# Two Mamba stages and a ConvLSTM: the first direction's softplus summed on TensorE, B and C spread through DRAM, five pairs in two chunks with B on GpSimd

## The chip, the cores and the metric

The kernel runs on one core of a Trainium2 chip. The time is the device time of one execution in microseconds (us): 7586.24, the median of three runs (7583.68 to 7590.27). Engines are named as in the profile: PE (TensorE), DVE (VectorE), ACT (ScalarE), POOL (GpSimd), SP (SyncE, which here only issues transfers).

## The reference, cut to what matters

The input x is 1 x 64 x 256 x 128 in float32 (channels, time, frequency). Layer 0 runs two Mamba stages, one along time (L = 256) and one along frequency (L = 128), each with a forward and a backward direction. Layer 1, a convolutional LSTM, follows; the change doesn't touch it. For each sequence a direction computes, with d = 128 inner channels and 16 states s:

```python
xz = einsum(rmsnorm(u), in_proj);  x, z = split(xz)
x = silu(causal_conv4(x))
dt, B, C = split(einsum(x, x_proj), [4, 16, 16])
dt = softplus(einsum(dt, dt_proj) + dt_b)
for t:                                    # a scan along the sequence
    h = exp(dt[t] * A) * h + dt[t] * B[t] * x[t]      # h is d x s
    y[t] = sum_s(h * C[t])
out = einsum((y + x * Dp) * silu(z), out_proj) + u
```

## The kernel before

A stage works through 64 chunks of 512 tokens (2 sequences of 256, or 4 of 128). The 128 x 16 = 2048 rows of h of one direction are cut into 16 groups of 128 partitions (8 channels by 16 states). Two groups make a **pair**, a tile of 128 x 1024; a direction has 8 pairs, a chunk 16: pairs 0 to 7 of the first direction, 8 to 15 of the second. All engines run through one hand-written order (`run`, L561): a step S for every pair, and in it, in this order,

- `times_b(S + 1)` (L454): the PSUM tile `bx` times B, on DVE. For the pairs in `SWAPPED` (L61, numbers modulo 32, so over two chunks) ACT copies `bx` to the SBUF tile `dA` and writes the decays into `bx` instead, and POOL does the product[...]
- `recur(S)` (L464): the scan itself, one DVE instruction of 128 x 1024; after the last pair of a direction `gate` (L509), y times silu(z) on DVE
- `outputs(S - 1)` (L482): h times C on POOL
- `inputs(S + 2)` (L421): four pairs of matmuls that spread dt * x to the rows of the pair, into one of three `bx` tiles
- `decays(S + 2)` (L435): ACT's exp(A * rep), two instructions, into one of four `dA` tiles; in slot 5 of a chunk the decays of S + 2 and of S + 3 are done, in slot 6 none
- what `HEAD` (L68) has for this slot
- `add_up(S - 2)` (L487), every second step: PE sums h * C over the states.

`HEAD` is the list of what prepares a chunk: (slot, function, arguments). Slots count steps from the first pair of the chunk **before** the one prepared; slot 16 is the prepared chunk's first pair, and a slot of 18 or -4 falls together with slot 2 or 12 of the neighbouring chunk. The steps of one slot run in the list's order, an older chunk's ahead of a younger one's. Each engine takes its own instructions strictly in this order.

The way of one chunk through `HEAD`: `squares`, `means`, `rms`, `normalise` (L305: xn on POOL, then four transfers of 64 KB into `unp`, SBUF to SBUF); `project_x` and `project_z` on PE, ACT copies to `xs` and `zs`; `silus` (L340) in slot 5 with a change of ACT's table before and after; then for each direction d

- `softplus_a`, `softplus_b` (L349, L363): the matmul with Wdt, then six ACT passes. `softplus_c`, `softplus_d`: dt = relu + log w + (e + w), three adds on POOL
- `dt_away` (L380): dt to DRAM (`there`), four transfers of 64 KB
- `spread_dt` (L400): four times 1 MB from `there` to `rep`, where a partition holds the dt of its channels; three `rep` tiles, each used by two pairs
- `times_x` (L387): dtx = dt * xs on POOL
- `project_bc` (L392): B and C, already spread over 128 partitions, by matmuls with weights in which each of the 16 columns stands eight times, and ACT copies from PSUM.

All transfers are issued by SP, in this same order. Matmuls of the head share one PSUM tile (`mm`, L273), so each waits until ACT has read the one before.

Of the kernel before, what the change touches and what calls it, by code (L numbers as in the profile page):

```python
# [29 lines left out]
F32 = mybir.dt.float32  # L30
# [6 lines left out]
P = 128  # L37
# [3 lines left out]
NS = 16  # L41
NBC = 2 * NS
DL = P // NS
# [3 lines left out]
NTOK = 512  # L47
# [10 lines left out]
NRING = 4  # L58
NH = 5
LAG = 2  # L60
SWAPPED = (5, 21, 29)  # L61
EXP_AND_LN = "natural_log_exp_and_others"
SILU = "silu_and_others"
EDGES = (0, 1, LF - 2, LF - 1)
# [2 lines left out]

HEAD = (  # L68
    (-12, "load"),
    (-7, "squares"),  # L70
    (-6, "means"),
    (-6, "rms"),
    (-6, "normalise"),
    (0, "project_x", 0),
    (1, "project_z", 0),
    (4, "project_x", 1),
    (5, "project_z", 1),
    (5, "silus"),
    (7, "softplus_a", 0),
    (7, "softplus_b", 0),  # L80
    (9, "softplus_c", 0),
    (9, "project_bc", 0, 1),
    (10, "softplus_d", 0),
    (10, "dt_away", 0),
    (11, "softplus_a", 1),
    (11, "spread_dt", 0, 0),
    (12, "times_x", 0),
    (12, "project_bc", 1, 1),
    (12, "project_bc", 0, 0),
    (12, "spread_dt", 0, 1),  # L90
    (13, "softplus_b", 1),
    (13, "project_bc", 1, 0),
    (14, "spread_dt", 0, 2),
    (15, "softplus_c", 1),
    (16, "softplus_d", 1),
    (16, "spread_dt", 0, 3),
    (17, "dt_away", 1),
    (18, "spread_dt", 1, 0),
    (20, "times_x", 1),
    (20, "spread_dt", 1, 1),  # L100
    (22, "spread_dt", 1, 2),
# [4 lines left out]
class Mamba:  # L106


    def __init__(self, ctx, tc, d):
        nc = tc.nc  # L110
        self.nc, self.tc = nc, tc
        cp = ctx.enter_context(tc.tile_pool(name="m_const", bufs=1))
# [47 lines left out]
        nc.scalar.activation(self.A, self.A, AF.Exp)  # L160
        nc.vector.tensor_scalar(self.A, self.A, -1.0, None, ALU.mult)

        self.G1, self.G2, self.Wz, self.Wdt, self.Wb, self.Wc, self.Dd, self.W2 = ([] for _ in range(8))
        self.W3, self.lin_b = [], []
        with tc.tile_pool(name="m_prep", bufs=2) as pp, tc.tile_pool(
            name="m_prep_ps", bufs=2, space=PSUM
        ) as ps:
            lins = []
            for i, n in enumerate(("tlin", "flin")):
                lin = pp.tile([C, 2, C], F32, name=n, tag=n, bufs=1)  # L170
                nc.sync.dma_start(out=lin, in_=d[n + "_w"].rearrange("(h i) o -> i h o", h=2))
                lins.append(lin)
                b = cp.tile([C, 1], F32, name=n + "b", tag=n + "b")
                nc.sync.dma_start(out=b, in_=d[n + "_b"].rearrange("(c o) -> c o", o=1))
                self.lin_b.append(b)

                w3 = cp.tile([P, 2, C], F32, name=f"w3{i}", tag=f"w3{i}")
                nc.vector.memset(w3, 0.0)
                nc.vector.tensor_add(w3[0:C, 0], lin[:, 0], lin[:, 1])
                nc.vector.tensor_add(w3[0:C, 0], w3[0:C, 0], self.ident[0:C, 0:C])  # L180
                nc.vector.tensor_copy(w3[C:P, 1], w3[0:C, 0])
                self.W3.append(w3)

            for i in range(4):
                win = pp.tile([C, 2 * P], F32, name="win", tag="win")
                nc.sync.dma_start(out=win, in_=d["in_proj"][i])
                cw = pp.tile([C, 4, P], F32, name="cw", tag="cw")
                nc.sync.dma_start(out=cw, in_=d["conv_w"][i].partition_broadcast(C))
                xpd = pp.tile([RANK, P], F32, name="xpd", tag="xpd")
                nc.sync.dma_start(out=xpd, in_=d["x_proj_dt"][i])  # L190
                dtw = pp.tile([RANK, P], F32, name="dtw", tag="dtw")
                nc.sync.dma_start(out=dtw, in_=d["dt_proj"][i])
                xbc = pp.tile([P, NBC], F32, name="xbc", tag="xbc")
                nc.sync.dma_start(out=xbc, in_=d["x_proj_bc"][i])
                ow = pp.tile([C, P], F32, name="ow", tag="ow")
                nc.sync.dma_start(out=ow, in_=d["out_proj"][i])

                nc.vector.tensor_scalar(win, win, normw[:, i : i + 1], None, ALU.mult)
                wz = cp.tile([C, P], F32, name=f"wz{i}", tag=f"wz{i}")
                nc.vector.tensor_copy(wz, win[:, P : 2 * P])  # L200
                self.Wz.append(wz)

                taps = ((3, 2), (1, 0)) if i % 2 == 0 else ((2, 3), (0, 1))
                for j, keep in enumerate((self.G1, self.G2)):
                    g = cp.tile([P, P], F32, name=f"g{j}{i}", tag=f"g{j}{i}")
                    nc.vector.tensor_mul(g[0:C], win[:, 0:P], cw[:, taps[j][0]])
                    nc.vector.tensor_mul(g[C:P], win[:, 0:P], cw[:, taps[j][1]])
                    keep.append(g)

                pw = ps.tile([P, P], F32, name="pw", tag="pw")  # L210
                nc.tensor.matmul(pw, lhsT=xpd, rhs=dtw, start=True, stop=True)
                wdt = cp.tile([P, P], F32, name=f"wdt{i}", tag=f"wdt{i}")
                nc.vector.tensor_copy(wdt, pw)
                self.Wdt.append(wdt)

                for h, keep in ((0, self.Wb), (1, self.Wc)):
                    w = cp.tile([P, NS, DL], F32, name=f"wbc{h}{i}", tag=f"wbc{h}{i}")
                    nc.vector.tensor_copy(
                        w, xbc[:, h * NS : (h + 1) * NS].unsqueeze(2).to_broadcast([P, NS, DL])
                    )  # L220
                    keep.append(w.rearrange("p s d -> p (s d)"))

                dd = cp.tile([P, P], F32, name=f"dd{i}", tag=f"dd{i}")
                nc.vector.tensor_scalar(dd, self.ident, dp[:, i : i + 1], None, ALU.mult)
                self.Dd.append(dd)

                po = ps.tile([P, C], F32, name="po", tag="po")
                nc.tensor.matmul(po, lhsT=ow, rhs=lins[i // 2][:, i % 2], start=True, stop=True)
                w2 = cp.tile([P, C], F32, name=f"w2{i}", tag=f"w2{i}")
                nc.vector.tensor_copy(w2, po)  # L230
                self.W2.append(w2)


class Stage:
# [142 lines left out]
    def softplus_d(self, ch, d):  # L377
        self.nc.gpsimd.tensor_add(self.at["dt", d], self.at["lw", d], self.at["dt", d])  # L378

    def dt_away(self, ch, d):  # L380

        there = self.dram.tile([32, 4, NTOK], F32, name="there", tag="there")
        for r in range(4):
            self.nc.sync.dma_start(out=there[:, r], in_=self.at["dt", d][32 * r : 32 * r + 32])
        self.at["there", ch, d] = there
# [3 lines left out]
        self.nc.gpsimd.tensor_mul(dtx, self.at["dt", d], self.at["xs", ch, d])  # L389
        self.at["dtx", ch, d] = dtx  # L390

    def project_bc(self, ch, d, h):  # L392
        wt = (self.m.Wb, self.m.Wc)[h][2 * self.stage + d]
        pb = self.mm("pb")
        self.nc.tensor.matmul(pb, lhsT=wt, rhs=self.at["xs", ch, d], start=True, stop=True)  # L395
        t = self.wk.tile([P, NTOK], F32, name="bc", tag=f"bc{h}", bufs=3)
        self.nc.scalar.copy(t, pb)  # L397
        self.at["BC"[h], ch, d] = t

    def spread_dt(self, ch, d, k):  # L400
# [28 lines left out]
        self.at["bx", S] = bx  # L429

    def swapped(self, S):

        return S % 32 in SWAPPED

# [711 lines left out]
```

## Time and profile before

| engine | busy us | share | what most of it is |
|---|---|---|---|
| DVE | 7263.6 | 96% | scans (L472) and products with B (L462) |
| POOL | 6916.1 | 91% | h times C (L485) 4806.7, B of swapped pairs (L459) 453.5, four softplus and dtx passes of about 327 each |
| PE | 6523.0 | 86% | bx (L428), sums over states (L500), B and C (L395) 655.8 |
| ACT | 5568.8 | 73% | decays (L450), copies of B and C (L397) 294.4 |
| transfers | - | 68.9% of 16 engines | rep (L403), 1024 of 1 MB |

The two Mamba stages fill the span up to about 6900 us, the ConvLSTM the rest. A line of a group reads: line, engine, operation, output<-input, shapes, count; busy us and mean ns of one; idle time ahead of it, and what ended it. In a timeline a line reads: start in us from the span's start, duration (of a merged row: from its first start to its last end), engine, line, operation, count, and in brackets how long the engine was idle and for what. SPq is SP's queue of transfers; its rows show the issue, not the landing.

### The profile page before, as it was taken

Reading aid. Unit: us, or ns where it says so; the run is one execution under the profiler, and the core shown is the slowest. Engines: PE = TensorE matmul, PEld = TensorE weight load, DVE = VectorE, ACT = ScalarE, POOL = GpSimd, SP = SyncE. Lnnn points to the kernel's source line nnn. Section 1 sums busy time; section 2 is a strip of 40 time slices with the busy share of each in tenths; the row PEclk is TensorE's granted clock in tenths of the full one; section 3 lists DMA queues with packets and bytes.
Section 4 is the critical chain, followed back from the end, with each engine's and each line's share of the span. In section 5 each row is a group of like instructions: output and inputs, shape, how many; then the busy total and the mean of one; then the engine's idle time right before and its main releaser. Section 6 shows DMA issues by size and latency. Waiting matters only on the chain.

```text
span 7581.6 us, 83087 instructions
## 1 busy us (share of the span) xinstructions
PE 6523.0 (86%) x24588; PEld 2179.7 (29%) x24588; DVE 7263.6 (96%) x5008; ACT 5568.8 (73%) x10188; POOL 6916.1 (91%) x3860
## 2 busy tenths in 40 slices
PE   6888888888888888887988888888888888888999
PEld 2222222222222222221222222222222222225887
DVE  6999999999999999997999999999999999996887
ACT  5778777777777877775787877878778787774333
POOL 6999999999999999996999999999999999995554
PEclk9999999999999999998999999999999999999999
DMA  5777877777777777775778777777777777772000
GB/s 131 175 178 175 183 174 177 174 174 182 176 181 174 174 182 177 180 173 124 184 182 186 171 176 172 171 181 172 178 173 171 179 171 179 172 172 77 15 15 17
DMA packets 276049, 1208.67 MB, mean 159 GB/s; under 512 B 46704, under 2 KB 104720, under 8 KB 144528
## 3 DMA queue, kind: packets, MB, share of 16 engines
q1 hardware_dynamic: 275600, 1203.35, 68.9%
q8 instruction: 200, 3.28, 0.2%
q14 instruction: 249, 2.04, 0.1%
HBM read 1094.12 MB, written 75.50 MB: 154 GB/s over the span
## 4 chain that ended last, share of the span: by engine, by line
PE 21%; ACT 10%; issue 9%; DVE 6%; DMA 5%; POOL 4%; SPq 0%; POOLq 0%; DVEq 0%; ACTq 0%
PE cv L911 6%; DVE h L472 5%; PE bx L428 4%; DMA rep<-there 4%; ACT dA L450 3%; POOL h L485 3%; PE y L500 2%; PE pb L395 2%; DVE bx L462 1%; PE y L493 1%; ACT L342 1%; PE pg L967 1%; PE px L322 1%; ACT L347 1%; PE both L1023 1%
## 5 line engine op out<-in xcount | busy, mean ns | idle before, releaser
L485 POOL TENSOR_TENSOR h<-h,bc 128x1024 f32<-128x1024 f32 x2048 | 4806.7, 2365 | 179.0 <-DVE h L472 167.7
L472 DVE TENSOR_TENSOR_SCAN h<-dA,bx 128x1024 f32<-128x1024 f32 x1856 | 4205.5, 2275 | 0.7 <-POOL e L374 0.7
L428 PE MATMUL bx<-dtx,sel 64*128 64x512 f32 x8192 | 2371.3, 654 | 755.2 <-DVE h L472 736.0
L450 ACT ACTIVATE dA<-rep,A 128x510 f32<-128x510 f32 (+1 forms) x3712 | 2461.6, 713 | 453.7 <-DMA rep<-there 439.9
L462 DVE TENSOR_TENSOR bx<-bx,bc 128x1024 f32<-128x1024 f32 x1856 | 2245.9, 1210 | 117.0 <-PE bx L428 116.0
L428 PEld LDWEIGHTS bx<-dtx,sel 64*128 64x128 f32 x8192 | 648.2, 189 | 2390.1 <-issue 1093.5
L500 PE MATMUL y<-h,fold 128*32 128x512 f32 x8192 | 1272.4, 638 | 25.9 <-POOL h L485 22.9
L395 PE MATMUL pb<-xs,wbc 128*128 128x512 f32 x1024 | 655.8, 726 | 119.8 <-ACT bc L397 112.8
L444 ACT COPY dA<-bx 128x1024 f32<-128x1024 f32 x192 | 194.4, 1012 | 474.7 <-PE bx L428 472.4
L500 PEld LDWEIGHTS y<-h,fold 128*32 128x32 f32 x8192 | 185.6, 111 | 969.8 <-issue 455.2
L459 POOL TENSOR_TENSOR dA<-dA,bc 128x1024 f32<-128x1024 f32 x192 | 453.5, 2362 | 5.6 <-ACT dA L444 5.6
L397 ACT COPY bc<-pb 128x512 f32<-128x512 f32 x512 | 294.4, 575 | 218.2 <-PE pb L395 218.2
L472 DVE TENSOR_TENSOR_SCAN h<-bx,dA 128x1024 f32<-128x1024 f32 x192 | 438.4, 2283 | 12.6 <-POOL dA L459 10.8
L374 POOL TENSOR_TENSOR e<-e,w 128x512 f32<-128x512 f32 x256 | 327.1, 1278 | 68.8 <-ACT w L369 68.4
L375 POOL TENSOR_TENSOR lw<-lw,e 128x512 f32<-128x512 f32 x256 | 326.0, 1273 | 20.1
L389 POOL TENSOR_TENSOR dtx<-dt,xs 128x512 f32<-128x512 f32 x256 | 327.4, 1279 | 0.0
L378 POOL TENSOR_TENSOR dt<-lw,dt 128x512 f32<-128x512 f32 x256 | 326.6, 1276 | 0.3
L395 PEld LDWEIGHTS pb<-xs,wbc 128*128 128x128 f32 x1024 | 166.9, 205 | 554.3 <-ACT bc L397 318.9
L322 PE MATMUL px<-unp,g 128*128 128x512 f32 x512 | 291.4, 650 | 31.3 <-ACT X L544 17.8
L324 ACT ACTIVATE xs<-px,cb 128x512 f32<-128x512 f32 x256 | 175.4, 685 | 175.9 <-PE px L323 173.9
L355 PE MATMUL pv<-xs,wdt 128*128 128x512 f32 x512 | 294.1, 657 | 12.0 <-ACT xs L346 9.9
L329 PE MATMUL pz<-unp,wz 64*128 64x512 f32 x512 | 271.0, 609 | 9.0 <-ACT xs L324 8.8
(187 smaller groups left out, 6983.0 us busy)
## 6 DMA issues: line engine op xcount, KB each, us to landing
rep<-there SPq DMA_DIRECT2D x1024, 1024.0 KB
there<-dt SPq DMA_DIRECT2D x1024, 64.0 KB
unp<-xn SPq DMA_DIRECT2D x512, 64.0 KB
u<-in_x SPq DMA_DIRECT2D x128, 64.0 KB
out<-y SPq DMA_DIRECT2D x32, 256.0 KB
w<-in_W_ih_f SPq DMA_DIRECT2D x10, 512.0 KB
w<-in_W_ih_b SPq DMA_DIRECT2D x10, 512.0 KB
cw<-in_conv_w SPq DMA_DIRECT2D x4, 128.0 KB
```

The source lines that it names most:

```text
L322: nc.tensor.matmul(self.seqs(px), lhsT=m.G1[i], rhs=self.unp[:, :, first : first + L], start=True, stop=False)
L374: self.nc.gpsimd.tensor_add(e, e, w)
L389: self.nc.gpsimd.tensor_mul(dtx, self.at["dt", d], self.at["xs", ch, d])
L395: self.nc.tensor.matmul(pb, lhsT=wt, rhs=self.at["xs", ch, d], start=True, stop=True)
L428: self.nc.tensor.matmul(bx[:, j], lhsT=self.m.sel[rows, r, k], rhs=dtx[rows], start=True, stop=True)
L450: nc.scalar.activation(dA[:, j, :, live], self.seqs(rep[:, r + 2 * j])[:, :, live], AF.Exp, scale=m.A[:, i, g : g + 1])
L459: self.nc.gpsimd.tensor_mul(bx, bx, b)
L462: self.nc.vector.tensor_mul(bx, bx, b)
L472: self.nc.vector.tensor_tensor_scan(h.rearrange("p j n -> p (j n)")[:, step], dA[:, step], bx[:, step], 0.0, ALU.mult, ALU.add,)
L485: self.nc.gpsimd.tensor_mul(h, h, self.at["C", ch, d].unsqueeze(1).to_broadcast([P, 2, NTOK]))
L500: nc.tensor.matmul(y[32 * r : 32 * r + 32], lhsT=m.fold[:, k], rhs=hs[r % 2][:, r // 2], start=False, stop=k == NK - 1, skip_group_check=True,
L911: self.nc.tensor.matmul(t[:, g, :, 0:n_out], lhsT=wts[s][:, gate * P : (gate + 1) * P], rhs=self.parts[n][:, :, s : s + n_out], start=s == ...
```

## The change

It takes work off DVE and POOL and gives some to PE and to the transfers. Two more of 32 pairs have their product with B on POOL. To make room there, the three softplus adds of the first direction become four matmuls with the identity that accumulate in PSUM, and an ACT copy (`softplus_sum`). B and C are projected once to 32 rows, copied by ACT, written to DRAM (`away`), and read back spread over 128 partitions (`spread_bc`), so that PE and ACT do two operations in place of four. `HEAD` is laid out anew; `normalise` goes from slot -6 to -4.

```diff
@@ -58,7 +58,7 @@
 NRING = 4
 NH = 5
 LAG = 2
-SWAPPED = (5, 21, 29)
+SWAPPED = (4, 10, 15, 21, 29)
 EXP_AND_LN = "natural_log_exp_and_others"
 SILU = "silu_and_others"
 EDGES = (0, 1, LF - 2, LF - 1)
@@ -67,35 +67,36 @@
 
 HEAD = (
     (-12, "load"),
-    (-7, "squares"),
-    (-6, "means"),
-    (-6, "rms"),
-    (-6, "normalise"),
+    (-8, "squares"),
+    (-5, "means"),
+    (-5, "rms"),
+    (-4, "normalise"),
     (0, "project_x", 0),
     (1, "project_z", 0),
     (4, "project_x", 1),
     (5, "project_z", 1),
     (5, "silus"),
-    (7, "softplus_a", 0),
-    (7, "softplus_b", 0),
-    (9, "softplus_c", 0),
-    (9, "project_bc", 0, 1),
-    (10, "softplus_d", 0),
+    (7, "project_bc", 0),
+    (8, "softplus_a", 0),
+    (8, "softplus_b", 0),
+    (10, "spread_bc", 0, 0),
+    (10, "softplus_sum", 0),
     (10, "dt_away", 0),
-    (11, "softplus_a", 1),
+    (11, "times_x", 0),
     (11, "spread_dt", 0, 0),
-    (12, "times_x", 0),
-    (12, "project_bc", 1, 1),
-    (12, "project_bc", 0, 0),
+    (12, "project_bc", 1),
     (12, "spread_dt", 0, 1),
+    (13, "softplus_a", 1),
     (13, "softplus_b", 1),
-    (13, "project_bc", 1, 0),
+    (13, "spread_bc", 1, 0),
     (14, "spread_dt", 0, 2),
+    (14, "spread_bc", 0, 1),
     (15, "softplus_c", 1),
+    (16, "spread_dt", 0, 3),
     (16, "softplus_d", 1),
-    (16, "spread_dt", 0, 3),
     (17, "dt_away", 1),
     (18, "spread_dt", 1, 0),
+    (18, "spread_bc", 1, 1),
     (20, "times_x", 1),
     (20, "spread_dt", 1, 1),
     (22, "spread_dt", 1, 2),
@@ -160,7 +161,7 @@
         nc.scalar.activation(self.A, self.A, AF.Exp)
         nc.vector.tensor_scalar(self.A, self.A, -1.0, None, ALU.mult)
 
...
         self.W3, self.lin_b = [], []
         with tc.tile_pool(name="m_prep", bufs=2) as pp, tc.tile_pool(
             name="m_prep_ps", bufs=2, space=PSUM
@@ -190,8 +191,9 @@
                 nc.sync.dma_start(out=xpd, in_=d["x_proj_dt"][i])
                 dtw = pp.tile([RANK, P], F32, name="dtw", tag="dtw")
                 nc.sync.dma_start(out=dtw, in_=d["dt_proj"][i])
-                xbc = pp.tile([P, NBC], F32, name="xbc", tag="xbc")
+                xbc = cp.tile([P, NBC], F32, name=f"xbc{i}", tag=f"xbc{i}")
                 nc.sync.dma_start(out=xbc, in_=d["x_proj_bc"][i])
+                self.Wbc.append(xbc)
                 ow = pp.tile([C, P], F32, name="ow", tag="ow")
                 nc.sync.dma_start(out=ow, in_=d["out_proj"][i])
 
@@ -212,13 +214,6 @@
                 wdt = cp.tile([P, P], F32, name=f"wdt{i}", tag=f"wdt{i}")
                 nc.vector.tensor_copy(wdt, pw)
                 self.Wdt.append(wdt)
-
-                for h, keep in ((0, self.Wb), (1, self.Wc)):
-                    w = cp.tile([P, NS, DL], F32, name=f"wbc{h}{i}", tag=f"wbc{h}{i}")
-                    nc.vector.tensor_copy(
-                        w, xbc[:, h * NS : (h + 1) * NS].unsqueeze(2).to_broadcast([P, NS, DL])
-                    )
-                    keep.append(w.rearrange("p s d -> p (s d)"))
 
                 dd = cp.tile([P, P], F32, name=f"dd{i}", tag=f"dd{i}")
                 nc.vector.tensor_scalar(dd, self.ident, dp[:, i : i + 1], None, ALU.mult)
@@ -377,6 +372,15 @@
     def softplus_d(self, ch, d):
         self.nc.gpsimd.tensor_add(self.at["dt", d], self.at["lw", d], self.at["dt", d])
 
+    def softplus_sum(self, ch, d):
+
+        nc = self.nc
+        ps = self.mm("ps")
+        parts = [self.at[n, d] for n in ("dt", "e", "w", "lw")]
+        for n, t in enumerate(parts):
+            nc.tensor.matmul(ps, lhsT=self.m.ident, rhs=t, start=n == 0, stop=n == len(parts) - 1)
+        nc.scalar.copy(self.at["dt", d], ps)
+
     def dt_away(self, ch, d):
 
         there = self.dram.tile([32, 4, NTOK], F32, name="there", tag="there")
@@ -389,12 +393,22 @@
         self.nc.gpsimd.tensor_mul(dtx, self.at["dt", d], self.at["xs", ch, d])
         self.at["dtx", ch, d] = dtx
 
-    def project_bc(self, ch, d, h):
-        wt = (self.m.Wb, self.m.Wc)[h][2 * self.stage + d]
-        pb = self.mm("pb")
-        self.nc.tensor.matmul(pb, lhsT=wt, rhs=self.at["xs", ch, d], start=True, stop=True)
-        t = self.wk.tile([P, NTOK], F32, name="bc", tag=f"bc{h}", bufs=3)
+    def project_bc(self, ch, d):
+
+        pb = self.mm("pb")[0:NBC]
+        self.nc.tensor.matmul(pb, lhsT=self.m.Wbc[2 * self.stage + d], rhs=self.at["xs", ch, d], start=True, stop=True)
+        t = self.wk.tile([NBC, NTOK], F32, name="bc", tag="bc")
         self.nc.scalar.copy(t, pb)
+        away = self.dram.tile([NBC, NTOK], F32, name="away", tag="away")
+        self.nc.sync.dma_start(out=away, in_=t)
+        self.at["away", ch, d] = away
+
+    def spread_bc(self, ch, d, h):
+        t = self.wk.tile([P, NTOK], F32, name="BC"[h], tag="BC"[h], bufs=3)
+        away = self.at["away", ch, d]
+        self.nc.sync.dma_start(
+            out=t, in_=away[NS * h : NS * (h + 1)].unsqueeze(1).to_broadcast([NS, DL, NTOK])
+        )
         self.at["BC"[h], ch, d] = t
 
     def spread_dt(self, ch, d, k):
@@ -429,6 +443,7 @@
         self.at["bx", S] = bx
 
     def swapped(self, S):
+
 
         return S % 32 in SWAPPED
```

More of the change, by code (lines that the diff above doesn't have):

```diff
@@ L161, in __init__ @@
         nc.vector.tensor_scalar(self.A, self.A, -1.0, None, ALU.mult)
-        self.G1, self.G2, self.Wz, self.Wdt, self.Wb, self.Wc, self.Dd, self.W2 = ([] for _ in range(8))
+        self.G1, self.G2, self.Wz, self.Wdt, self.Wbc, self.Dd, self.W2 = ([] for _ in range(7))
         self.W3, self.lin_b = [], []
```

## Prediction

> **What bounds the kernel now.** I read the page first: busy shares and costliest groups.
>
> ```profile
> PE 6523.0 (86%) x24588; PEld 2179.7 (29%) x24588; DVE 7263.6 (96%) x5008; ACT 5568.8 (73%) x10188; POOL 6916.1 (91%) x3860
> ...
> L472 DVE TENSOR_TENSOR_SCAN h<-dA,bx 128x1024 f32<-128x1024 f32 x1856 | 4205.5, 2275 | 0.7 <-POOL e L374 0.7
> ...
> L462 DVE TENSOR_TENSOR bx<-bx,bc 128x1024 f32<-128x1024 f32 x1856 | 2245.9, 1210 | 117.0 <-PE bx L428 116.0
> ```
>
> VectorE (DVE) is busy 96% of the span, GpSimd (POOL) 91%; each of DVE's scans takes 2275 ns, each of its B products 1210 ns. The share over stretches inside the two Mamba stages says more:
>
> ```profile
> 1812.00:2368.00 556.00, 478.71 (x1760) 129.89 (x1759) 554.87 (x344) 433.06 (x778) 542.34 (x280) 0.98 0.79 179
> ```
>
> The columns are busy time of PE, weight load, DVE, ACT and POOL, then clock, DMA share, GB/s. DVE works 554.87 of 556 us. In the table of waits DVE waits 116.0 us for PE in the whole run, 48.7 of them once. So in a chunk DVE sets the pace, and a cut in DVE's work pays in full only if no other dependency takes as long as DVE does now. The gate products, one per direction (start times 2013.12 and 2066.13, 2040.19 and 2092.42), give a chunk of 53.0 and 52.2 us, on average 52.6.
>
> The other candidate is a loop that runs from one chunk to the next, which I read from the timeline (start, us, engine, operation):
>
> ```profile
> 2014.32 1.28 POOL L378 TENSOR_TENSOR dt<-lw,dt 128x512 f32<-128x512 f32 x1
> ...
> 2015.63 1.72 SPq L384 DMA_DIRECT2D there<-dt  x4
> ...
> 2017.46 2.42 SPq L311 DMA_DIRECT2D unp<-xn  x4
> ...
> 2020.06 10.71 SPq L403 DMA_DIRECT2D rep<-there  x4
> ...
> 2027.58 1.33 ACT L450 ACTIVATE dA<-rep,A 128x510 f32<-128x510 f32 x2 [1.95 <-DMA rep<-there]
> ...
> 2032.33 1.33 ACT L450 ACTIVATE dA<-rep,A 128x510 f32<-128x510 f32 x2 [2.01 <-DMA rep<-there]
> ...
> 2035.70 1.72 SPq L384 DMA_DIRECT2D there<-dt  x4
> ...
> 2042.52 2.19 SPq L403 DMA_DIRECT2D rep<-there  x2
> ...
> 2049.76 1.33 ACT L450 ACTIVATE dA<-rep,A 128x510 f32<-128x510 f32 x2
> ...
> 2066.96 1.28 POOL L378 TENSOR_TENSOR dt<-lw,dt 128x512 f32<-128x512 f32 x1
> ```
>
> The first direction's dt ends at 2015.60 (2014.32 + 1.28). It goes to DRAM, `unp` is copied, and the first `rep` is issued at 2020.06. The reps land 4.75 us apart (2027.58, 2032.33: ACT starts as they land): the transfer engines are full, at 217 to 221 GB/s in stretches of 2 us. The second direction's dt is written from 2035.70, but its first rep is issued only at 2042.52: the write stood behind the reps. ACT uses that rep at 2049.76, in slot 5, just ahead of the silus that the next chunk's softplus needs; that chunk's dt ends at 2068.24. The sum is 4.46 + 22.46 + 7.24 + 18.48 = 52.64 us: **one chunk, the same as DVE's**. ACT gets to 2049.76 without waiting; in other chunks it waits 0.16 to 0.5 us at this place. This loop has almost no slack.
>
> **What the Trainium skill says.** "DMA: Bandwidth & Descriptors", section on queues, rings and completion order: each transfer engine takes descriptors in ring order. The trace agrees: 5.1 us from the last dt write's issue (2037.42) to the rep that waits for it. The same page, anatomy of one DMA: a wait happens on the issuing sequencer, so what is queued behind a waiting SyncE transfer waits too, and the landing receipt is most of a fixed 2 us. Here the data stop at 2041.75 and the rep is issued at 2042.52: 0.77 us, which I use. "GPSIMD Engine Reference", performance versus the Vector engine: an elementwise product is about 1.96 times slower there; the trace has 2365 against 1210 ns.
>
> **The change part by part, per chunk.**
> - *Swapped pairs 3 to 5 in 32*: one product more on POOL. Ordinary scans start 3.31 us apart (2018.14, 2021.45, 2024.76); two scans with no product between take 4.45, or 2.2 each. So DVE loses 1.1 us: 52.6 to 51.5. POOL gains 2.36, ACT one copy of 1.01 and a zero fill of 0.19.
> - *First softplus*: three POOL adds go (3 x 1.277 = 3.83), so POOL falls by 1.47 to some 49.8 us (542.34/556 of 52.6 is 51.3). PE gains four identity products. A pair of instructions takes 1.12 us (Wdt), a following pair 1.02: 4.1 us. ACT gains a copy of 0.58.
> - *B and C*: PE loses four products and gets two (-2.2), ACT four copies for two (-1.15). With the above PE goes from 45.3 (478.71/556) to 47.2, ACT from 41.0 to 41.6. No engine but DVE comes near 51.5.
> - *New transfers*: two writes of 64 KB and four spreads of 256 KB, 1.18 MB or 5.3 us at 221 GB/s. At a share of 0.79 the transfers fill 41.5 of 52.6 us, then 46.8. Not the sum matters, but where it falls. The first direction's B and the second C and the writes near them lie outside the loop. Inside it, ahead of the second direction's first rep, now stand: the second `away` write (64 KB), the second B and first C (256 KB each), and `unp` (256 KB), which at slot -4 moves from before the first rep to behind the second. 832 KB at 221 GB/s is 3.85 us, at the 260 GB/s of short 2 KB or 1 KB bursts (dt at 2041, unp) 3.3: I take 3.6. Bounds: 2.8 (the best half microsecond, 300 GB/s) and 6.4 (twice the packet cost, no such queue being in the trace).
> - *Waits added*: the second B spread waits on SyncE for its write, which stands behind the first rep; behind it wait two reps, the first C and the dt write. The second rep is in the ring by then and keeps it full until after the wait: nothing. The setup loses eight DVE copies (under 2 us), and the first chunk of a stage gains a DRAM round trip of some 2 us: taken as even.
>
> **The loop after.** (a) dt ready to first rep: unp is out of the way. Data of the dt write flowed until 2018.2, 2.6 after dt, plus 0.77: 3.35 instead of 4.46. (b) to the second direction's first rep: 22.46 + 3.6 = 26.1. (c) landing 7.24. (d) ACT from those decays to the new dt. Before: first decays to the end of softplus_b 11.7 (2049.76 to 2061.45). Now `project_bc` at slot 7 puts a copy (0.6) in, softplus at slot 8 comes behind one more pair's decays (1.4), then follow the square (0.35), two pairs' decays (2.75) and the dt copy (0.6): 17.4. In even chunks pair 10 is swapped, and its copy adds 1.1: 18.5; mean 17.95. PE's sum (inputs 1.2, then 4.1) ends about as ACT gets there. Total 3.35 + 26.1 + 7.24 + 17.95 = **54.6 us**, against 51.5 of DVE. So DVE will wait 3 us a chunk for ACT, and a chunk gets 2.0 us longer: 127 x 2.0 = 254, and 7586 + 254 = **7840 us**.
>
> **Rivals.**
> 1. *DVE stays the bound.* Some step of the loop has slack that I don't see (POOL's adds start 0.6 us after ACT's last input is ready, 2062.05 against 2061.45; the rep need not be so late). For it: DVE's 99.8%, and all busy sums fall below 51.5. 7586 - 128 x 1.1 = 7445. Chance 0.20.
> 2. *The product of x waits for unp.* PE's projection at slot 0 stands ahead of the bx inputs that DVE needs. unp lands behind the second rep: 3.35 + 7.5 + 4.75 + 1.4 = 17.0 after dt; projection and inputs take 3.4; DVE from there to the scan at slot 9 takes 26.0 (2036.88 to 2062.9), inputs, sum and copy 6.05. This loop has 52.5 us: against DVE's 51.5 it eats the gain, about 7575. It would rule if the ACT loop is shorter than I think. Chance 0.15.
> 3. *The same loop, larger*: the short packets cost 5.5 instead of 3.6 in a full ring, or a lagging transfer engine delays landing (a stage 1 chunk shows its first rep 9.15 us after issue). 56.5 us, 7586 + 127 x 3.9 = 8080. Chance 0.15.
> Mine, 0.50: with its lower bound (2.8 for the transfers: 53.8) 7740, upper about 7950.
>
> **Range and chances.** I leave out a few per cent below rival 1's value and the upper half of rival 3: 7440 to 7990. Faster takes rival 1 and half of rival 2: 0.27; same 0.05; slower 0.68.
>
> **What would show it.** Right: gates of one direction 54 to 55 us apart; DVE's share in a stage window down to some 94% with its idle time ended by ACT's decays; ACT's wait for reps up from 440 us by 2 to 4 us a chunk, most of it at slot 5; the second dt write to its rep longer than 6.8 us. Steps: dt to first rep 3.4 us; the unp copies after the second rep's issue. Wrong: ACT not waiting at slot 5, or DVE still at 99% in the windows with chunks of 51.5 (rival 1); PE's projection waiting for unp with DVE waiting for bx (rival 2). The forecast falls if the transfers don't keep ring order, or if the slot 5 decays don't stand ahead of the silus in ACT's queue.

## The result, and the profile after

| kernel | median us (runs) | ratio to before, 95% interval |
|---|---|---|
| before | 7587.08 (4) | 1 |
| changed | 7768.18 (4), 7757.71 to 7778.82 | 1.0239, 1.0221 to 1.0257 |

The changed kernel is 181 us slower. The forecast had 254 us slower. The page of the changed kernel, busy time and the costliest group:

```profile
PE 6703.1 (86%) x25100; PEld 2266.2 (29%) x25100; DVE 7137.2 (92%) x4872; ACT 5656.8 (73%) x10316; POOL 6731.9 (87%) x3604
...
L500 POOL TENSOR_TENSOR h<-h,C 128x1024 f32<-128x1024 f32 x2048 | 4795.0, 2364 | 515.3 <-DMA C<-away 318.7
```

The same stretch of a stage as before (PE, weight load, DVE, ACT, POOL, clock, DMA share, GB/s):

```profile
1812.00:2368.00 556.00, 484.20 (x1761) 132.81 (x1760) 531.00 (x326) 430.29 (x769) 513.33 (x253) 0.98 0.85 196
```

DVE had 554.87 of these 556 us; now it has 531.00 and waits for the rest. No other engine is near 100%, so nothing has become a bound by its load. What does DVE wait for? Lines of the table of waits (engine, line, releaser: us in total, times, longest):

```profile
POOL h L500 <- DMA C<-away: 318.7, 101, 10.7
...
DVE bx L477 <- PE bx L442: 284.1, 187, 44.3
ACT dA L465 <- DMA rep<-there: 235.0, 217, 3.3
...
PE px L317 <- DMA unp<-xn: 169.5, 96, 9.3
...
DVE h L487 <- POOL dA L474: 136.0, 104, 4.4
...
DVE h L487 <- ACT dA L465: 9.3, 8, 3.7
```

DVE's own three lines are an account that closes. Its busy time fell by 126.4 us (7263.6 to 7137.2). Its wait for PE's `bx` rose by 168.1 (116.0 to 284.1), for POOL's swapped products by 125.2 (10.8 to 136.0), for ACT's decays by 9.3. The sum is +176.2; the spans of the two profiles differ by 176.6 (7581.6 and 7758.2). **So the saving came in full and DVE gave it back more than twice over, waiting for PE and POOL, and hardly ever for ACT.** What those two waited for is above and below DVE's lines: POOL for the first direction's C, PE for `unp`.

The timeline of one chunk, dt to dt (rows of other work left out; transfers of SPq are issues):

```profile
2007.83 0.58 ACT L382 COPY dt<-ps 128x512 f32<-128x512 f32 x1 [0.54 <-PE ps L381]
2008.44 1.71 SPq L388 DMA_DIRECT2D there<-dt  x4
...
2011.53 0.52 SPq L417 DMA_DIRECT2D rep<-there  x1
...
2014.45 0.52 SPq L417 DMA_DIRECT2D rep<-there  x1
...
2015.39 3.33 SPq L306 DMA_DIRECT2D unp<-xn  x4
...
2019.71 0.55 SPq L409 DMA_DIRECT2D B<-away  x1
...
2020.36 0.55 SPq L417 DMA_DIRECT2D rep<-there  x1
...
2020.95 0.59 SPq L409 DMA_DIRECT2D C<-away  x1
...
2025.56 1.85 PE L317 MATMUL px<-unp,g 128*128 128x512 f32 x2 [1.80 <-DMA unp<-xn]
...
2028.47 1.70 SPq L388 DMA_DIRECT2D there<-dt  x4
...
2031.99 4.67 POOL L500 TENSOR_TENSOR h<-h,C 128x1024 f32<-128x1024 f32 x2 [3.54 <-DMA C<-away]
...
2036.42 0.52 SPq L417 DMA_DIRECT2D rep<-there  x1
2036.61 2.37 POOL L474 TENSOR_TENSOR dA<-dA,B 128x1024 f32<-128x1024 f32 x1
...
2039.01 2.29 DVE L487 TENSOR_TENSOR_SCAN h<-bx,dA 128x1024 f32<-128x1024 f32 x1 [1.42 <-POOL dA L474]
...
2044.09 1.33 ACT L465 ACTIVATE dA<-rep,A 128x510 f32<-128x510 f32 x2
...
2061.57 0.58 ACT L382 COPY dt<-ps 128x512 f32<-128x512 f32 x1
```

Follow C. It is issued at 2020.95, behind two reps, `unp`, B and a third rep, and POOL can use it only at 2031.99, 11 us later, having stood for 3.54 us. The product of pair 4 stands behind the first two h times C in POOL's queue (2036.61), and DVE's scan of pair 4 waits for it (2039.01). ACT's slot 5 decays, which the forecast took for the end of the loop, start at 2044.09 with no wait in brackets. In other chunks ACT does wait there (0.42 us at 2096.57; 0.5 us on average in the 37 chunks from 1000 to 3000 us; in the kernel before 0.2, and up to 0.97, where the prediction names 0.16 to 0.5), so one chunk doesn't settle what binds; an edit has to. Further up, PE's projection of x waits 1.80 us for `unp`; that is the forecast's second rival, alive beside it.

### The profile page after: what moved, and what is told of

It is laid out like the page before. It is cut to its first block, busy times and chain, and to the rows that moved or that the text cites. A ratio compares the mean times of both kernels' runs of the same rounds, so it can differ in the third digit from the quotient of the medians.

```text
span 7758.2 us, 84989 instructions
## 1 busy us (share of the span) xinstructions
PE 6703.1 (86%) x25100; PEld 2266.2 (29%) x25100; DVE 7137.2 (92%) x4872; ACT 5656.8 (73%) x10316; POOL 6731.9 (87%) x3604
## 4 chain that ended last, share of the span: by engine, by line
PE 16%; DMA 10%; issue 9%; DVE 8%; POOL 5%; ACT 5%; SPq 1%; POOLq 0%; DVEq 0%; ACTq 0%
DVE h L487 6%; PE cv L926 6%; POOL h L500 3%; PE bx L442 3%; DMA rep<-there 3%; DMA C<-away 2%; DMA unp<-xn 2%; DMA there<-dt 2%; DVE bx L477 2%; PE ps L381 1%; ACT dA L465 1%; PE y L515 1%; POOL dA L474 1%; PE pg L982 1%; PE both L1038 1%
## 5 line engine op out<-in xcount | busy, mean ns | idle before, releaser
L500 POOL TENSOR_TENSOR h<-h,C 128x1024 f32<-128x1024 f32 x2048 | 4795.0, 2364 | 515.3 <-DMA C<-away 318.7
L487 DVE TENSOR_TENSOR_SCAN h<-dA,bx 128x1024 f32<-128x1024 f32 x1728 | 3906.0, 2273 | 9.3 <-ACT dA L465 9.3
L465 ACT ACTIVATE dA<-rep,A 128x510 f32<-128x510 f32 (+1 forms) x3456 | 2275.5, 710 | 239.2 <-DMA rep<-there 235.0
L477 DVE TENSOR_TENSOR bx<-bx,B 128x1024 f32<-128x1024 f32 x1728 | 2094.3, 1212 | 284.9 <-PE bx L442 284.1
L487 DVE TENSOR_TENSOR_SCAN h<-bx,dA 128x1024 f32<-128x1024 f32 x320 | 730.4, 2283 | 136.5 <-POOL dA L474 136.0
L474 POOL TENSOR_TENSOR dA<-dA,B 128x1024 f32<-128x1024 f32 x320 | 756.3, 2364 | 32.0 <-ACT dA L459 27.1
L317 PE MATMUL px<-unp,g 128*128 128x512 f32 x512 | 323.5, 717 | 251.8 <-DMA unp<-xn 169.5
L465 ACT ACTIVATE bx<-rep,A 128x510 f32<-128x510 f32 (+1 forms) x640 | 441.0, 689 | 21.2 <-ACT bx L462 0.4
L399 PE MATMUL pb<-xs,xbc 128*32 128x512 f32 x512 | 288.2, 647 | 19.2 <-ACT xs L341 17.4
L318 PE MATMUL px<-unp,g 128*128 128x512 f32 x512 | 304.7, 681 | 0.0
L508 PE MATMUL y<-xs,dd 128*128 128x512 f32 x512 | 276.4, 622 | 0.0
L324 PE MATMUL pz<-unp,wz 64*128 64x512 f32 x512 | 265.5, 598 | 3.1 <-ACT xs L319 3.1
```

The costliest lines, as they stand in the source:

```text
L317: nc.tensor.matmul(self.seqs(px), lhsT=m.G1[i], rhs=self.unp[:, :, first : first + L], start=True, stop=False)
L318: nc.tensor.matmul(self.seqs(px), lhsT=m.G2[i], rhs=self.unp[:, :, second : second + L], start=False, stop=True)
L465: nc.scalar.activation(dA[:, j, :, live], self.seqs(rep[:, r + 2 * j])[:, :, live], AF.Exp, scale=m.A[:, i, g : g + 1])
L474: self.nc.gpsimd.tensor_mul(bx, bx, b)
L477: self.nc.vector.tensor_mul(bx, bx, b)
L487: self.nc.vector.tensor_tensor_scan(h.rearrange("p j n -> p (j n)")[:, step], dA[:, step], bx[:, step], 0.0, ALU.mult, ALU.add,)
```

## The experiments

Three theories. **A**, the forecast's: the loop from chunk to chunk closes at ACT's decays in slot 5, which wait for the second direction's first rep. **B**, its second rival: `unp` lands late, PE projects late, `bx` is late. **C**, new: the first C lands late, POOL's products queue up behind it, DVE waits for the swapped ones. Each run was timed beside the kernel before on the same chip (whose medians were then 7582.0 to 7586.9 us); runs of different series are best compared by their ratios.

### unp one slot earlier

```diff
-    (-4, "normalise"),
+    (-5, "normalise"),
```

> The changed kernel with normalise one slot earlier (slot -5 in place of -4), so that the four unp copies are issued between the first rep and the second, not behind the second. The bytes ahead of the second direction's first rep stay the same. If ACT's slot 5 decays hold the chunk (the forecast's loop), nothing moves: 7740 to 7790 us. If PE's projection of x waiting for unp holds it (rival 2), DVE's excess waits for PE (284 us here against 116 before) go: 7600 to 7660 us, and PE's 169 us of waiting for unp fall below 30. If POOL's wait for C holds it, little moves: 7720 to 7770 us, with the wait for C as it was (319 us) or longer.

7770.59 us, ratio 1.0246 (1.0230 to 1.0261). PE's wait for `unp` fell from 169.5 to 20.5 us and nothing was gained: DVE's wait for `bx` fell by 35 us (to 249.4) and the one for swapped products rose by 41 (to 176.6). The time lies in A's band and 0.6 us above C's. POOL's wait for C was shorter (232.5), not as long as before as C's reading had it, but its xn now waited 197.9 us for ACT's `rs` (38.6 in the changed kernel). B alone isn't the cause.

### The first C beside its B

```diff
     (10, "spread_bc", 0, 0),
+    (10, "spread_bc", 0, 1),
...
-    (14, "spread_bc", 0, 1),
```

> The changed kernel with the first direction's C spread issued beside its B at slot 10, ahead of the dt write, in place of slot 14 behind the third rep. It leaves the queue ahead of the second direction's first rep by 256 KB. Forecast's loop: 1.15 us a chunk shorter, 7610 to 7640 us. Rival 2 (unp): unp lands as before, 7740 to 7770 us. POOL's wait for C: its 319 us go, and DVE's 136 us of waiting for the swapped product with them: 7630 to 7680 us.

7649.37 us, ratio 1.0089 (1.0074 to 1.0104): 67 us above the kernel before beside it, where the changed kernel was 181 above. **So moving one transfer of 256 KB gave 114 of the 181 us.** In the timeline C now stands ahead of the dt write and of the reps of its direction. It is first used seven steps later, some 30 us after its issue; there POOL's products, the swapped one of pair 4 and DVE's scan of it follow with no wait in brackets:

```profile
2020.68 0.51 SPq L409 DMA_DIRECT2D B<-away  x1
...
2021.23 0.60 SPq L409 DMA_DIRECT2D C<-away  x1
...
2028.56 1.73 SPq L388 DMA_DIRECT2D there<-dt  x4
...
2048.92 6.99 POOL L500 TENSOR_TENSOR h<-h,C 128x1024 f32<-128x1024 f32 x3
...
2055.87 2.34 POOL L474 TENSOR_TENSOR dA<-dA,B 128x1024 f32<-128x1024 f32 x1
...
2059.29 2.28 DVE L487 TENSOR_TENSOR_SCAN h<-bx,dA 128x1024 f32<-128x1024 f32 x1
```

The groups of this kernel show the swapped scans without idle time ahead of them; it was 136.5 us:

```profile
L487 DVE TENSOR_TENSOR_SCAN h<-bx,dA 128x1024 f32<-128x1024 f32 x320 | 729.4, 2279 | 0.0
```

As many bytes move as in the changed kernel; only one transfer has changed its place in the queue. The same edit also takes 256 KB from ahead of the second direction's first rep, so A forecast a gain too. But the time is 9 us above A's band and inside C's, ACT's wait for reps rose (235.0 to 266.7), and the gain is DVE's wait for swapped products, while its wait for `bx` stayed (284.1 and 288.7). C is shown.

### Both

> Both edits: unp between the first and the second rep, and the first direction's C at slot 10. Forecast's loop: as the C edit alone, 7610 to 7640 us. If the waits for unp and for C are the two causes, both go, DVE is the bound again at 51.5 us a chunk or the slot 5 loop at some 53: 7450 to 7640 us, and clearly below either edit alone.

7624.47 us, ratio 1.0052 (1.0036 to 1.0069): 25 us less than with C alone. The value lies in both bands; the step of 25 us is what A has no room for. DVE's wait for `bx` fell by 118 us against the run with C alone (288.7 to 170.9), but a wait of 116.0 us for swapped products came back, for another reason, which the timeline of this kernel shows:

```profile
2079.71 0.42 ACT L298 ACTIVATE rs<-rs 128x256 f32<-128x256 f32 x1
...
2080.20 0.73 POOL L303 TENSOR_TENSOR xn<-u,rs 128x256 f32<-128x256 f32 x1 [2.69 <-ACT rs L298]
2080.89 2.35 POOL L474 TENSOR_TENSOR dA<-dA,B 128x1024 f32<-128x1024 f32 x1
...
2083.28 2.29 DVE L487 TENSOR_TENSOR_SCAN h<-bx,dA 128x1024 f32<-128x1024 f32 x1 [1.87 <-POOL dA L474]
```

xn, one slot earlier, reaches POOL before ACT has made `rs`; POOL stands 2.69 us, and the product of pair 15 behind it comes 1.87 us late for DVE, in every second chunk (62 times in the run).

### The silus ahead of the slot 5 decays

```diff
-            for ahead in ((2, 3) if S % 16 == silu else () if S % 16 == silu + 1 else (2,)):
+            for ahead in (2,):
```

> The changed kernel with the decays of a direction's first pair behind the silus (slot 6), not ahead of them (slot 5), so that the silus and the next softplus no longer stand behind the second direction's first rep. Forecast's loop: cut, dt of the next chunk some 1.4 us or more earlier, 7560 to 7680 us. Rival 2 and the wait for C: unchanged or a little earlier, 7730 to 7790 us.

On the changed kernel: 7754.21 us, ratio 1.0223 (1.0208 to 1.0239), 14 us less, with intervals that overlap; POOL's wait for C (322.9) and DVE's two waits (280.6 and 135.4) as they were. A's closing point was not what bound the changed kernel.

> The changed kernel with unp written one slot earlier, the first direction's first C spread beside its B (slot 10 instead of 14), and in addition the slot 5 decays behind the silus. Without this last edit it took 7624 us, with VectorE at 94%. A (ACT's loop that closes at slot 5 is the next bound): ACT waits there for the second direction's first rep ahead of the silus, up to 1.5 us in the chunk I read; taken out of the chain to dt it gives 0.5 to 1.2 us a chunk, so 7470 to 7560. C (what is left is VectorE's wait for bx and for the swapped product of pair 15, and neither hangs on the silus): 7600 to 7640.

On top of the two moved transfers the same edit gives 62 us: 7562.49 us, ratio 0.9969 (0.9957 to 0.9981). That is 2.5 us above A's band and 38 below C's. The gain is in DVE's wait for `bx` (170.9 to 123.2). So ACT's slot 5 does limit the kernel once C is early, as A has it. How much of that is the rep is not shown: the edit takes two things from ahead of the silus, the wait for the rep (1.51 us at 2057.53 in the kernel without this edit) and the 1.33 us of the decays themselves.

### Where unp stands when the rest is mended

> The changed kernel with the first C at slot 10 and the slot 5 decays behind the silus, unp where the change puts it (normalise at slot -4). It tells whether the late unp still costs when the other two chains are out of the way. Against 7562 with the early unp. B (unp late, then TensorE's projection, then bx: the forecast's second rival, 52.5 us a chunk): VectorE waits for bx by 200 us or more, 7575 to 7640. If unp has slack: xn at slot -4 no longer stands ahead of the swapped product of pair 15, and it is 7440 to 7520.

7581.22 us, ratio 0.9995 (0.9986 to 1.0004), inside B's band: with `unp` late PE waits 199.7 us for it and DVE 254.8 for `bx`. An early `unp` is worth 19 us here (7581 to 7562), with the wait of pair 15 that it brings already taken off. The run also says where the silus edit belongs: against C alone (1.0089 to 0.9995) it gives some 70 us with `unp` still late. It stood behind C and not behind `unp`; the two gains add up, in either order.

### Means and rms earlier

```diff
-    (-5, "means"),
-    (-5, "rms"),
+    (-6, "means"),
+    (-6, "rms"),
```

> The changed kernel with unp one slot earlier and the first C at slot 10, and in addition the means and the rms one slot earlier (slot -6 instead of -5, as in the kernel before), so that GpSimd's xn no longer waits for ACT's rs ahead of the swapped product of pair 15. C carried on (swapped products held up on GpSimd are what VectorE waits for): VectorE's wait for them falls from 116 us to under 40, and the time from 7624 to 7520 to 7570. A: no effect, 7610 to 7640; or slower, if the square and rms displace ACT's softplus.

7613.24 us, ratio 1.0037 (1.0025 to 1.0049), 11 us less than without the edit (the intervals overlap) and not the 55 to 105 that C expected; it lies in the other band. The wait for swapped products went as expected, but DVE's wait for `bx` rose from 170.9 to 266.1: the wait had moved.

> All four edits on the changed kernel: unp at slot -5, first C at slot 10, slot 5 decays behind the silus, means and rms at slot -6. Without the last edit: 7562 us, VectorE at 98.2%, and its only waits in two chunks are 0.16 and 1.88 us (the swapped product of pair 15, held up because GpSimd's xn waits for rs). Taken alone: 63 x 1.9 = 120 us less, 7445, which is also what VectorE as the only bound gives. But with the slot 5 decays ahead of the silus the same edit only moved the wait: VectorE waited 1.1 us a chunk for bx, because the means product stands on TensorE, behind ACT's copy of dt, ahead of the bx inputs. If that holds here too: 7540 to 7610.

With the silus first as well: **7543.70 us, ratio 0.9953 (0.9936 to 0.9971), the fastest kernel of the study**, 0.5% under the kernel before and in the band of a wait that only moves. Two of its five runs (7564 and 7567 us) are no faster than the kernel without the last edit (7562), so that step of 19 us is not sure. The wait moved here too (`bx` 123.2 to 220.0), by less than it had taken away. Its timeline shows where:

```profile
2057.69 0.58 ACT L382 COPY dt<-ps 128x512 f32<-128x512 f32 x1 [1.91 <-PE ps L381]
...
2058.33 0.70 PE L292 MATMUL pm<-sq,ones 128*128 128x256 f32 x2 [0.68 <-ACT dt L382]
...
2058.96 1.13 PE L442 MATMUL bx<-dtx,sel 64*128 64x512 f32 x4
...
2063.25 1.23 DVE L477 TENSOR_TENSOR bx<-bx,B 128x1024 f32<-128x1024 f32 x1 [1.11 <-PE bx L442]
```

The means product and the sum of dt use the same PSUM tile `mm`, so PE waits for ACT's copy of dt before it can go on, and the `bx` inputs stand behind it.

```diff
-    (-8, "squares"),
-    (-6, "means"),
-    (-6, "rms"),
+    (-9, "squares"),
+    (-8, "means"),
+    (-8, "rms"),
```

> The changed kernel with C at slot 10, the slot 5 decays behind the silus, xn at slot -5, and square, means and rms taken out of the way of the dt sum: square at slot -9, means and rms at slot -8, right behind the softplus inputs. In the kernel with means and rms at slot -6 (7544 us) the means product waited 0.68 us on TensorE for ACT's copy of dt, ahead of the bx inputs, and VectorE waited 0.51 to 1.11 us a chunk for bx. If the order on TensorE and ACT around slot 10 is all that is left: VectorE at 99% in the windows and 7450 to 7490. If the rms ahead of slot 9's decays lengthens the way to dt instead: 7540 to 7600, with VectorE waiting for bx or for ACT's decays.

7872.83 us, ratio 1.0375 (1.0361 to 1.0390): a miss of both bands. The wait grew with the move:

```profile
2033.39 0.70 PE L292 MATMUL pm<-sq,ones 128*128 128x256 f32 x2 [2.38 <-ACT dt L354]
...
2038.72 1.12 PE L381 MATMUL ps<-dt,ident 128*128 128x512 f32 x2
```

Right behind Wdt's product the means product needs the tile that ACT's two passes are still reading; PE stood 2.38 us, then the `bx` inputs, the sums over states and the dt sum followed late. DVE's wait for `bx` is 547.5 us. I had looked at the order on each queue and not at who holds the one tile.

### Parts of the change on the kernel before

```diff
-SWAPPED = (5, 21, 29)
+SWAPPED = (4, 10, 15, 21, 29)
```

> The kernel before with five swapped pairs (4, 10, 15, 21, 29) instead of three, and nothing else of the change. It tells what the VectorE saving is worth with no new transfer and GpSimd at some 52.4 us a chunk (50.6 was 91% of the span; two products of 2.36 us per two chunks more). If VectorE alone sets the chunk: 127 x 1.1 us less, 7445. If the ACT loop of the forecast, without slack at 52.6 us, also holds: no gain, 7570 to 7600. If GpSimd becomes the bound: 7560 to 7650 and VectorE waits for swapped products.

7910.89 us, ratio 1.0428 (1.0413 to 1.0444), slower than any of the three bands. The window and a wait of this kernel:

```profile
1812.00:2368.00 556.00, 474.65 (x1670) 127.50 (x1674) 520.35 (x317) 426.36 (x765) 538.13 (x278) 0.95 0.74 169
```

```profile
DVE h L472 <- POOL dA L459: 289.4, 242, 2.6
```

POOL works 538.13 of 556 us: with a chunk of 52.6 + 326 / 127 = 55.2 us that is 53.4, where 51.3 (before) + 2.36 makes 53.7. POOL now needs more than the old chunk of 52.6 us, and DVE waits for its swapped products 242 times. By its load alone that explains about 1 us a chunk, 100 to 140 of the 326 us; DVE's wait for `bx` rose as well (116.0 to 262.9), and the rest stays open. (The 52.4 in the expectation started from the share of the whole span; the window's 51.3 is the right start.) Two more swapped pairs alone can't pay: POOL has no room for them until the softplus adds have gone.

> The kernel before with five swapped pairs and the first direction's softplus summed on TensorE (sum and dt copy at slot 10), B and C made by matmul as before, so no new transfer and no C that lands late. C (the late first C is what cost the change its time): VectorE comes back to 96% or more and the time is at or under that of the kernel before, 7450 to 7590. A rival: TensorE's extra 4.1 us a chunk (some 49.4 of 51.5 us) makes bx late, VectorE waits for bx by 150 us or more, and it is 7600 to 7700.

Edit: the five pairs, and `softplus_sum` in slot 10 in place of `softplus_c` and `softplus_d` of the first direction. 8060.66 us, ratio 1.0624 (1.0606 to 1.0642), a miss of both. POOL has room (495.46 of 556 us in the window), but:

```profile
POOL xn L307 <- ACT rs L302: 664.3, 128, 35.2
...
DVE bx L470 <- PE bx L436: 531.6, 326, 49.9
```

> The kernel before with five swapped pairs, the sum on TensorE and the changed kernel's slots for square, means, rms and xn (-8, -5, -5, -4), B and C still by matmul. In the run with the old slots GpSimd's xn waited 664 us for rs, which stands on ACT behind the copy of dt that waits for TensorE's sum. If that was the cost: 8061 falls to 7600 to 7750 and the wait for rs under 200 us. If it is TensorE's load and its one bank for products (softplus, B, C, sum and means one after another): little change, 7950 to 8070, with VectorE's wait for bx still near 530 us.

8361.23 us, ratio 1.1020 (1.1003 to 1.1036), above both bands. The wait for `rs` fell to 56.5 us as the first reading wanted, and the time rose by 300. So taking that wait away did not help: in its place PE's means product now waits 265.5 us for ACT's softplus passes to leave the tile (85.1 us for the dt copy in the run before this one). DVE's wait for `bx` is 791.0, the second reading's sign, though well above the 530 it named. ACT waits 482.2 us for B and C products (218.2 in the kernel before) and 372.2 for dt sums; in the changed kernel it is 91.0 and 81.6. All of these go through the tile `mm`; that they queue there is my reading, no run gave them a second tile, and PE's greater load is not ruled out. If it holds, it says what the way through DRAM is for: it takes two of the four B and C products of a chunk off that tile.

## Why the prediction was right, and where it was not

DVE's time in the profiles of the main kernels, all in us. "Rest" is what is left of the span, DVE idle for anything else, in the ConvLSTM and at the ends:

| kernel | span | DVE busy | waits: bx | swapped | decays | rest |
|---|---|---|---|---|---|---|
| before | 7581.6 | 7263.6 | 116.0 | 10.8 | 0 | 191.2 |
| changed | 7758.2 | 7137.2 | 284.1 | 136.0 | 9.3 | 191.6 |
| first C early | 7643.4 | 7138.0 | 288.7 | 0 | 24.2 | 192.5 |
| and unp early | 7618.5 | 7124.6 | 170.9 | 116.0 | 15.6 | 191.4 |
| and silus first | 7561.1 | 7119.9 | 123.2 | 116.2 | 10.1 | 191.7 |
| and means at -6 | 7541.9 | 7120.7 | 220.0 | 0.8 | 8.8 | 191.6 |

The rest is the same to 1.3 us in all six, so the time is DVE's work plus its three waits, and each experiment reads as an entry of this table. The table shows where DVE stood; why the one it waited for was late takes the edits.

- **The saving**: 1.1 us a chunk forecast; 126.4 / 127 = 1.0 measured. Right.
- **The loads**: with a chunk of 52.6 + 181 / 127 = 54.05 us the window gives POOL 49.9 (forecast 49.8), PE 47.1 (47.2), ACT 41.8 (41.6), transfers 45.9 (46.8). Right, and none of them is what bound.
- **dt to the first rep**: 3.12 us (2008.41 to 2011.53; forecast 3.35). Right.
- **From there to the second direction's first rep**: 24.89 us (2011.53 to 2036.42), forecast 26.1. The term for 832 KB was mis-sized: 3.6 forecast, 24.89 - 22.46 = 2.4 measured. The second dt write takes 7.95 us to its rep (6.82 before): it stood behind the reps, as "DMA: Bandwidth & Descriptors", section on queues, rings and completion order, of the Trainium skill lets one expect. `unp` was issued after the second rep's issue, as said.
- **Two figures that the prediction quotes**: 1.96 is given for an addition of 2048 columns, not for a product; the products here show 2365 against 1210 ns, 1.95. The fixed 2 us is given for transfers that GpSimd issues; here SyncE issues them, and the sum rightly took the trace's 0.77 us instead.
- **To the decays and on to dt**: 7.67 and 18.06 us (forecast 7.24 and 17.95). All four terms make 53.74, against 54.6.
- **Where the loop closes**: wrong. Forecast: DVE waits 3 us a chunk for ACT, and ACT's wait for reps rises from 440 us by 2 to 4 us a chunk. Measured: DVE waits 9.3 us in all for ACT, and ACT's wait for reps *fell* to 235.0. The step that failed is "New transfers": it put the first C among the bytes ahead of the rep and never asked who waits for that C. "Waits added" named the second B's wait on SyncE, found nothing behind it, and left out that POOL's products, the swapped ones among them, hang on C.
- **The argument from the sum**: the forecast took "52.64, one chunk" as a sign of no slack. It is none: in a steady rhythm any way from one dt to the next sums to one chunk. The way through C and POOL in the timeline also makes 53.74 (2008.41 to 2031.99, 23.58; to the scan, 7.02; on to dt at 2062.15, 23.14). A wait in brackets at a link is a hint; what binds only an edit tells (ACT did wait at slot 5 in most chunks, and taking that out alone gained next to nothing).
- **Gates**: 53.8, 52.4, 53.1 and 54.1 us apart in one direction (from 2006.12 to 2219.56), on average 53.4 and a little under the 54 to 55 forecast; DVE's share in the window is 95.5% (forecast some 94%).
- **Rivals**: the second (late `unp`) was there and was worth 19 to 25 us, once C was out of the way (part of this may be the clock, see the last section). The first (DVE alone, 7445) was reached by no kernel; the nearest still waits 104 us more for `bx` than the kernel before. Taken out of the table it would stand at 7541.9 - 104 = 7438, an estimate that no run shows; as a floor the rival's number fits it. The third isn't needed.

So the side held for a reason close to the forecast's: new transfers that come late do cost more than DVE saves, 302.6 / 127 = 2.4 us a chunk in DVE's three waits (3.1 forecast). That the size came out near is luck, because the victim was another: first of all C, and beside it `unp`, which the change itself had put late. The forecast's own way, through ACT's slot 5, came next: it was worth next to nothing as long as C was late and 60 to 70 us after that.

## What to carry to other kernels

For a new transfer write down two things: what it delays, and who waits for it, with what stands behind that waiter on its engine; here one 256 KB spread four slots too late cost 114 us, at equal bytes and equal load. A path whose terms sum to the period proves nothing; look for the links with a wait, edit one at a time, and expect the next loops to sit just behind (first C, 114 us; then, in either order, the silus with 60 to 70 and `unp` with 19 to 25). Before moving an instruction to an earlier slot, check its engine's queue and the one buffer that it shares: three of the edits here took a wait away and set up another nearly as long.

## What the runs showed of the hardware

TensorE's granted clock differs between these kernels. In the same window it is 0.98 before, 0.95 with the five swaps alone, and 1.00 in the two fastest kernels; the matmul of `bx` takes 654, 668 and 644 to 648 ns. "TensorE: Matmul & The Clock Gate", part 1, of the Trainium skill says that idleness makes the hardware throttle the clock; here the steps are small and PE is busy 85 to 88% of the window in all of them.

Three pairs of kernels differ only in where `unp` stands, and in each of them every run with it early has the higher clock over the whole span:

| kernel | clock, `unp` late | clock, early | PE's wait for `unp`, us |
|---|---|---|---|
| changed | 0.964 to 0.968 | 0.980 to 0.981 | 169.5, 20.5 |
| first C early | 0.959 to 0.964 | 0.978 to 0.981 | 194.5, 11.8 |
| and silus first | 0.968 to 0.971 | 0.986 to 0.989 | 199.7, 11.8 |

So the clock goes with this stall of PE and not with the time: in the first pair the time is the same (7768 and 7771 us). What sets it no run tested. It also means that the 19 to 25 us of an early `unp` are not all shown to be the shorter wait; a part may be the faster clock that came with it.
